# A graph layer pair on one core: load order at the start, gathers one group earlier, rows moved from the edge loop to the node stage, destinations of the attention stage by six bits, and sums on GpSimd in the last stage

## The chip, the cores and the metric

The kernel runs on one core of a Trainium2 chip, in one launch. Its time is device microseconds; the median of three runs stands for a kernel. One further execution was profiled, and all durations below come from that one. Engines are named as in the profile: PE (TensorE), PEld (its weight loads), DVE (VectorE), ACT (ScalarE), POOL (GpSimd), SP (the queue that issues most DMAs).

## What is computed

6250 nodes of 128 features, 100,000 edges sorted by destination. First a message layer, then an attention layer, each with a residual and a layer norm:

```python
edge_features = concat([x[src], x[dst], gaussians(edge_weight)])
h = silu(edge_features @ Wm1 + bm1)
h = silu(h @ Wm2 + bm2)
out = segment_sum(h @ Wm3 + bm3, dst)
u = silu(concat([x, out]) @ Wu1 + bu1) @ Wu2 + bu2
x = layernorm(x + silu(u @ Wi1 + bi1) @ Wi2 + bi2)
xt = logmap0(x)
att = sigmoid(concat([xt[src], xt[dst], edge_attr_128]) @ att_w.T + att_b)
support = xt + segment_sum(xt[src] * att, src) + mean_by_src(edge_attr_128) + mean_by_dst(edge_attr_128)
x = layernorm(x + proj(expmap0(support)))
```

## The kernel before

`window_path` is the whole kernel; a second path exists for inputs that don't fit its windows and isn't run. The order of the instructions on each engine is written out by hand: every engine works through its own list, and waits on semaphores of the others. Edges go in 98 groups of 1024 (`NG`), a group in four windows of 256 and eight blocks of 128 edges.

**Start.** SP loads x in nine pieces (L889), ACT's queue the source and destination indices (L894), POOL's queue 17 weights and biases (L699, `later`, issued in one go). 13 rounds of four node blocks each are turned (L1014) and multiplied (L1033) once for `p_src`, once more for `p_dst`, the projections of all nodes; between them DVE works through `pieces`, a list that makes gather indices, window bases and low bits out of the raw indices.

**Edge loop** (L1270 on), two halves per group. `gather` (L1087) fetches the group's rows of `p_src` by eight indirect DMAs on POOL, two groups ahead of their use; 16 are issued before the loop. `layer1`, `layer2` and `sum_up` are the products (L1204, L1207, L1221, L1236). Rows of edge attributes have to be added by source node as well, and for this the kernel sorts them: `scatter` (L818) writes a block's 128 attribute rows by an indirect DMA into tables in HBM that have room for every block of 128 nodes (buckets). Of a group's eight blocks two are scattered in the edge loop (`early`, blocks 0 to 2), except that every fifth group leaves one of them for later (`left`, 20 groups); before its first scatter POOL waits for a copy of the low bits by ACT (`attr_row`, L1324).

**Node stage.** 13 rounds of four node blocks run the update network. `move_middle` scatters the third of blocks 0 to 2 of each group and then what `left` kept back, three rows a call: three SP loads, one to three ACT copies (L1359), three scatters. Each round calls it three times; what is left over comes after the rounds. After them a serial chain on DVE (L1476 to L1516) makes the logarithmic map's scale and `a_t`, the two dot products of every node with the attention weights. The destination's dot products are laid out for look-up as `w3`: for each of 392 windows, which begins at any node, a column of 128 values. Products with 0/1 matrices `up` fetch them out of `a_t` (L1526), a choice by `second` (is the low part of the base above the partition?) joins the two node blocks that a window reaches into (L1528 to L1531), and a loop splits it in three bf16 parts (L1533, L1535).

**Attention.** 98 iterations. In each, for group `it`: `logits` multiplies what was looked up with `hi` (`pick`, L1686), reduces it (L1687), adds the edge's own part (L1688), and ACT makes the sigmoids (L1689, L1692). `move` issues five scatters on POOL (L818) of blocks 3 to 7, whose rows now carry the sigmoid. `one_hots(it + 1)` makes `ohT` (L1663), a bf16 0/1 matrix of 128 partitions x 2048 columns: for each of 1024 edges the low seven bits of its source, then of its destination, compared with the partition number; and `hi` (L1665), which picks the node block. `look_up(it + 1)` has TensorE multiply them: for each of the eight blocks three products with the three parts of the source's table (L1677) and one with `w3` (L1679). The low bits arrive by one DMA of 512 KB that repeats a row of HBM over 128 partitions (`load_lo`, L1386). Beside that, sums of finished buckets are made from the tables (loads L1589, one-hots L1602, products L1618, `add` L1629), by a plan that spreads them over the iterations.

**Last stage.** Nine loads of the last buckets (`load(k)`, L1589, into four places, two used twice at first), for each `so_far` (L1794), one-hots (L1602), products (L1804), means (L1823), `xp` on POOL (L1830), its reduction (L1834); then, for blocks 0 to 23 and 24 to 48, `finish`: small products of 24 or 25 columns, and per block `scaled` on ACT (L1883), `added` on DVE (L1887) and a store for every six blocks.

Of the kernel before, what the change touches and what calls it, by code (L numbers as in the profile page):

```python
# [531 lines left out]
W = 64  # L532
# [17 lines left out]
def left(g):  # L550

    return (1, 2, 0)[g % 3] if g % 5 == 0 else None
# [50 lines left out]
def window_path(ctx, tc, bad, x, src, dst, edge_attr, edge_weight, Wm1, bm1, Wm2, bm2, Wm3, bm3,  # L603
# [49 lines left out]

    const = ctx.enter_context(tc.tile_pool(name="const", bufs=1))
# [36 lines left out]

    noff = const.tile([P, 1], F32, name="noff")
    nc.vector.tensor_scalar(noff, part, -float(KR), -STEP, op0=OP.add, op1=OP.mult)

# [3 lines left out]
    def later(t, w):  # L698
        waiting.append(lambda: nc.gpsimd.dma_start(t, w))  # L699
# [48 lines left out]

    wm3 = weight(Wm3, "wm3")
# [10 lines left out]
    later(bi2x, bi2[None, :].to_broadcast([P, F]))  # L760
    bi2p = const.tile([P, 4, F], BF16, name="bi2p")
# [11 lines left out]
    keep = ctx.enter_context(tc.tile_pool(name="keep", bufs=1))  # L773

# [9 lines left out]
    acc = keep.tile([P, 3, ROWS], F32, name="acc")  # L784
# [51 lines left out]
    egat = of_edges.enter_context(tc.tile_pool(name="egat", bufs=4, reuse_waits="tile"))  # L836
# [37 lines left out]
    with tc.tile_pool(name="init", bufs=1) as init, \  # L874
            tc.tile_pool(name="initw", bufs=3) as initw, \
            tc.tile_pool(name="initp", bufs=2, space=PSUM) as initp:

        xs = acc[:, 0, :NB * F].rearrange("p (r f) -> p r f", f=F)
        xT = acc[:, 2, :NB * P].rearrange("f (r p) -> f r p", p=P)
        XL = N - (P - 1) * NB  # L880
        xv = x[:(P - 1) * NB].rearrange("(p r) f -> p r f", r=NB)
        nc.vector.memset(xs[96:, XL:], 0.0)
# [4 lines left out]
        nc.vector.memset(raw[R0:, 1, TAIL:], -1)  # L887
        for lo, hi in ((0, 8), (8, 24), (24, NB)):
            nc.sync.dma_start(xs[:112, lo:hi], xv[:112, lo:hi])  # L889
            nc.sync.dma_start(xs[112:P - 1, lo:hi], xv[112:, lo:hi])  # L890
            nc.sync.dma_start(xs[P - 1:, lo:min(hi, XL)],
                              x[(P - 1) * NB + lo:(P - 1) * NB + min(hi, XL)][None])
        for s, v in enumerate((src, dst)):
            nc.scalar.dma_start(raw[:R0, s], v[:R0 * GE].rearrange("(g e) -> g e", e=GE))  # L894
            nc.scalar.dma_start(raw[R0:NG - 1, s], v[None, R0 * GE:(NG - 1) * GE])
            nc.scalar.dma_start(raw[NG - 1:, s, :TAIL], v[None, (NG - 1) * GE:])
        for f in waiting:
            f()
        for t in (p_src, p_dst):
            nc.sync.dma_start(t[NB * P:], zrow[:, :F])  # L900
        nc.sync.dma_start(first_t[(NB - 1) * LO:NB * LO].rearrange("(p r) f -> p r f", p=P),
                          zrow[:, None, :RW].to_broadcast([P, LO // P, RW]))
        nc.vector.memset(acc[:, 1], 0.0)
# [82 lines left out]
        def lower(s):  # L986
# [5 lines left out]
        pieces = [  # L992
# [6 lines left out]
            bases, spread, relative, lambda: turn(1), lambda: upper(0), lambda: upper(1), rest, begins,  # L999
            lambda: bias_rows(init, bm2x, bm2p),  # L1000
            lambda: nc.vector.tensor_copy(beside[:, 1:], attw),
            copy_lws,
            lambda: nc.vector.tensor_single_scalar(raw, raw, P - 1, OP.bitwise_and)]
# [17 lines left out]
        for s in range(2):  # L1021
            if s:
                load(0)
                load_attr(0)
                load(1)
            for r, (b0, nb) in enumerate(rounds):
                if s == 0:
                    turn_x(r + 1)
                if r % 2 == 0:
# [15 lines left out]
                if s or r >= 3:  # L1045
                    for _ in range(1):
                        if pieces:
                            pieces.pop(0)()
        for p_ in pieces:
            p_()  # L1050
        for s in range(2):
            lower(s)
# [5 lines left out]
    with tc.tile_pool(name="ework", bufs=2, reuse_waits="tile") as ework, \  # L1058
# [5 lines left out]

        counts = ework.tile([P, 2, NB], F32, name="counts", bufs=1)
# [14 lines left out]
        def gather(g, bs):  # L1080
            if g >= NG:
                return
            if g not in gas:
                gas[g] = egat.tile([P, 8, F], F32, name="ga")
# [193 lines left out]
        extra = {12: turn, 14: multiply, 16: lambda: bias_rows(ework, bi2x, bi2p)}  # L1278
# [3 lines left out]
        for g in range(2):  # L1282
# [6 lines left out]
        for g in range(NG + 2):  # L1289
            for half in range(2):  # L1290
# [10 lines left out]
                gather(g + 2, range(4 * half, 4 * half + 4))  # L1301
# [72 lines left out]

    w3 = stat.tile([P, 4 * NG, 3], BF16, name="w3")
# [7 lines left out]
    def load_lo(g):  # L1383
        if g < NG:
            los[g] = aload.tile([P, 2, 8, P], BF16, name="los")
            nc.sync.dma_start(los[g].rearrange("p s b e -> p (s b e)"),  # L1386
                              row_lo[g].rearrange("s e -> (s e)").partition_broadcast(P))

    with tc.tile_pool(name="nwork", bufs=2, reuse_waits="tile") as nwork, \
# [15 lines left out]
        up = nwork.tile([P, 2, NW], F32, name="up", bufs=1)  # L1405
        nc.vector.tensor_single_scalar(bits, base_w, P - 1, OP.bitwise_and)
        nc.vector.tensor_copy(bits_f, bits)
        nc.vector.tensor_scalar(second, bits_f, part, None, op0=OP.is_gt)
        nc.vector.tensor_single_scalar(bits, base_w, 7, OP.arith_shift_right)
        nc.vector.tensor_copy(bits_f, bits)  # L1410
        for q in range(2):
            nc.vector.tensor_scalar(up[:, q], bits_f, float(q), part, op0=OP.add, op1=OP.is_equal)
# [107 lines left out]
        a_up = stat.tile([NB, P], F32, name="a_up")  # L1520
        nc.vector.tensor_copy(a_up, pt[:NB, 0])
# [3 lines left out]
        for q, t in enumerate(two):  # L1525
            nc.tensor.matmul(t, lhsT=a_up, rhs=up[:NB, q], start=True, stop=True)  # L1526
# [5 lines left out]
        for q in range(3):  # L1532
            nc.vector.tensor_copy(w3[:, :, q], w_a)  # L1533
            if q < 2:
                nc.vector.tensor_sub(w_a, w_a, w3[:, :, q])  # L1535

# [35 lines left out]
    with tc.tile_pool(name="bwork", bufs=2, reuse_waits="tile") as bwork:  # L1572
# [58 lines left out]
        with tc.tile_pool(name="awork", bufs=2, reuse_waits="tile") as awork, \  # L1631
# [26 lines left out]
            def one_hots(g):  # L1658
# [3 lines left out]
                ohT = awork.tile([P, 2, 8, P], BF16, name="ohT")  # L1662
                nc.vector.tensor_scalar(ohT, los.pop(g), part, None, op0=OP.is_equal)  # L1663
# [320 lines left out]
```

## Time and profile before

| | us |
|---|---|
| median of three runs | 2843.29 (2835.01 to 2847.82) |
| profiled execution | 2827.59, its span 2825.8 |
| start, to the first layer-1 product | 0 to 68 |
| edge loop | 68 to 1683 |
| node stage | 1683 to 1886 |
| attention | 1886 to 2741 |
| last stage | 2741 to 2825.8 |

The mean granted TensorE clock of that execution was 0.754. A row of the profile names line, engine, operation, output and inputs by the program's names, and, in square brackets, how long the engine stood before it and what let it go; "issue" stands for a wait for nothing that the profile shows. The costliest groups, as count, busy time and mean duration:

```profile
L1087 POOL DMA_INDIRECT ga<-p_src,src_i x782 | 758.5, 970 | 261.6 <-issue 230.4
L818 POOL DMA_INDIRECT late<-attr,to_i x298 | 290.2, 974 | 253.0 <-ACT att L1692 143.5
L818 POOL DMA_INDIRECT early<-attr_row,to_i x176 | 175.5, 997 | 458.3 <-ACT attr_row L1324 269.6
L1677 PE MATMUL pg<-a,ohT 128*128 128x49 bf16 x2346 | 137.3, 199 | 200.2 <-DVE ohT L1663 102.6
```

A row reads: line, engine, operation, output and inputs, count; then busy time in us and mean duration in ns; then the idle time before, and what ended most of it.

### The profile page before, as it was taken

The page shows a single profiled execution, that of the slowest core. Times are in us where ns is not written, and L with a number is a line of the kernel's source. Part 1 is how long each engine was busy: PE and PEld are TensorE (multiplying, and loading weights), DVE is VectorE, ACT ScalarE, POOL GpSimd, SP SyncE. Part 2 cuts the span into 40 slices and gives each one's busy share as a digit, 9 for nine tenths or more (in the row PEclk, how much of TensorE's full clock was granted, in tenths as well). Part 3 has the DMA queues.
Part 4 walks back from the last instruction along what each step waited for, and adds up shares of the span by engine and source line. Part 5 has one row for each costly group of instructions (what it writes and reads, how often), then busy time and mean ns, then how long its engine had stood idle before and what let it go on. Part 6 is the DMA issues. An engine that isn't in the chain of part 4 may idle for free. (4 is left out here: it accounts for less than half of the span.)

```text
span 2825.8 us, 41692 instructions
## 1 busy us (share of the span) xinstructions
PE 1935.6 (68%) x13353; PEld 1678.1 (59%) x13353; DVE 1656.1 (59%) x4438; ACT 915.8 (32%) x1576; POOL 1550.3 (55%) x1608
## 2 busy tenths in 40 slices
PE   6567677776777675767777786746666776766674
PEld 5456566665666565656666673425555766666663
DVE  6466665666666555655666663444444555555668
ACT  3445444444444444444344431111111110000005
POOL 4556555555555555555655546545555555555542
PEclk8788878878777777878787786756666777676877
DMA  7445454454444444444433433446666666766743
GB/s 215 111 123 147 127 129 125 124 132 127 123 128 119 121 122 119 121 112 123 106 98 103 110 85 108 122 126 196 190 198 201 207 214 204 226 191 218 230 149 104
DMA packets 349749, 412.11 MB, mean 146 GB/s; under 512 B 53701, under 2 KB 265931, under 8 KB 349265
## 3 DMA queue, kind: packets, MB, share of 16 engines
q1 hardware_dynamic: 298168, 303.00, 37.9%
q0 software_dynamic: 50624, 105.02, 12.3%
q8 instruction: 108, 1.77, 0.3%
q10 hardware_dynamic: 728, 1.33, 0.2%
q14 instruction: 121, 0.99, 0.1%
HBM read 319.13 MB, written 90.00 MB: 145 GB/s over the span
## 5 line engine op out<-in xcount | busy, mean ns | idle before, releaser
L1087 POOL DMA_INDIRECT ga<-p_src,src_i x782 | 758.5, 970 | 261.6 <-issue 230.4
L1252 DVE TENSOR_TENSOR acc<-acc,ps 128x192 f32 x391 | 138.3, 354 | 511.2 <-remote 253.5
L818 POOL DMA_INDIRECT late<-attr,to_i x298 | 290.2, 974 | 253.0 <-ACT att L1692 143.5
L818 POOL DMA_INDIRECT early<-attr_row,to_i x176 | 175.5, 997 | 458.3 <-ACT attr_row L1324 269.6
L1618 PE MATMUL pb<-acc,oh 128*128 128x130 f32 x1764 | 348.5, 370 | 34.8 <-issue 33.9
L1236 PE MATMUL ps<-hot,h 128*128 128x64 f32 x1564 | 320.9, 285 | 73.7 <-issue 71.9
L1618 PEld LDWEIGHTS pb<-acc,oh 128*128 128x128 f32 x1764 | 322.4, 278 | 46.3 <-issue 45.7
L1210 ACT ACTIVATE h<-pa,bm1c 128x512 f32<-128x512 f32 x196 | 134.7, 687 | 648.1 <-remote 212.0
L1221 PEld LDWEIGHTS pb<-wm,h 128*128 128x128 f32 x1564 | 258.7, 232 | 102.7 <-issue 77.4
L1236 PEld LDWEIGHTS ps<-hot,h 128*128 128x128 f32 x1564 | 266.6, 211 | 75.4 <-issue 73.9
L1207 PE MATMUL pa<-feat,lw 128*128 128x256 f32 x782 | 278.4, 486 | 40.5 <-issue 38.6
L1221 PE MATMUL pb<-wm,h 128*128 128x128 f32 x1564 | 259.3, 313 | 50.7 <-issue 49.6
L1677 PE MATMUL pg<-a,ohT 128*128 128x49 bf16 x2346 | 137.3, 199 | 200.2 <-DVE ohT L1663 102.6
L1677 PEld LDWEIGHTS <-ohT 128*128 128x128 bf16 x2346 | 113.4, 105 | 232.5 <-DVE ohT L1663 115.1
L1238 PE MATMUL ps<-hot,attr 128*128 128x64 f32 x976 | 204.3, 286 | 54.6 <-issue 53.8
L1686 DVE TENSOR_TENSOR pick<-pg,hi 128x416 f32<-128x416 f32 x98 | 57.8, 590 | 309.3 <-remote 161.8
L1207 PEld LDWEIGHTS pa<-feat,lw 128*128 128x128 f32 x782 | 177.5, 250 | 82.0 <-issue 60.1
L1204 PE MATMUL pa<-ident,ga 128*128 128x128 f32 x782 | 162.8, 327 | 88.1 <-issue 52.1
L1238 PEld LDWEIGHTS ps<-hot,attr 128*128 128x128 f32 x976 | 161.6, 204 | 54.3 <-issue 53.9
L1223 ACT ACTIVATE h<-pb 128x512 f32<-128x512 f32 x196 | 116.4, 594 | 229.7 <-remote 111.7
L1204 PEld LDWEIGHTS pa<-ident,ga 128*128 128x128 f32 x782 | 113.2, 169 | 103.3 <-issue 75.2
L1689 ACT ACTIVATE attr<-lg,attb 128x5 f32<-128x5 f32 (+1 forms) x60 | 18.3, 305 | 412.9 <-DVE lg L1688 411.3
(343 smaller groups left out, 3995.5 us busy)
## 6 DMA issues: line engine op xcount, KB each, us to landing
los<-row_lo SPq DMA_DIRECT2D x98, 512.0 KB
near<-in_edge_weight_dram SPq DMA_DIRECT2D x97, 256.0 KB
attr<-in_edge_attr_dram SPq DMA_DIRECT2D x97, 256.0 KB
acc<-late SPq DMA_DIRECT2D x38, 528.0 KB
late<-zrow SPq DMA_DIRECT2D x22, 792.0 KB
acc<-early SPq DMA_DIRECT2D x49, 330.0 KB
attr<-in_edge_attr_dram SPq DMA_DIRECT2D x247, 64.0 KB
attr<-in_edge_attr_dram SPq DMA_DIRECT2D x118, 128.0 KB
```

Source lines behind the costliest of these rows:

```text
L818: nc.gpsimd.indirect_dma_start(out=t, out_offset=bass.IndirectOffsetOnAxis(ap=to_i[:, b, g:g + 1], axis=0), in_=rows_, in_offset=None)
L1087: nc.gpsimd.indirect_dma_start(out=gas[g][:, b], out_offset=None, in_=p_src[:, :], in_offset=bass.IndirectOffsetOnAxis(ap=src_i[:, b, g:g ...
L1204: nc.tensor.matmul(pa[:, j], lhsT=gas[g][:, 2 * k0 + j], rhs=ident, is_transpose=True, start=j == 0, stop=False)
L1207: nc.tensor.matmul(pa[:, 2 * k:2 * k + 2], lhsT=lws[(4 * g + k0 + k) % NL], rhs=feats[g][:, k0 + k], start=False, stop=k == kk - 1)
L1210: nc.scalar.activation(hid1[i][:, :2 * kk], pa[:, :2 * kk], AF.Silu, bias=bm1c)
L1221: nc.tensor.matmul(pb[:, j], lhsT=h1[:, j], rhs=wm2, start=False, stop=j == nb - 1)
L1223: nc.scalar.activation(hid2[i][:, :nb], pb[:, :nb], AF.Silu)
L1236: nc.tensor.matmul(ps[:, k, 0], lhsT=h2[:, 2 * k + c], rhs=hot[:, b], start=k == 0 and c == 0, stop=False)
L1238: nc.tensor.matmul(ps[:, k, 1], lhsT=head[:, b, :F] if b < 3 else rest[:, b - 3], rhs=hot[:, b], start=False, stop=False)
L1252: nc.vector.tensor_add(acc[:, :, bass.ds(at, W)], acc[:, :, bass.ds(at, W)], ps[:, k])
L1618: nc.tensor.matmul(pb[:, h], lhsT=oh[:, a + h, j], rhs=bt[:, a + h, j, :S], start=j == 0 and h == 0, stop=j == c - 1 and h == n - 1)
L1677: nc.tensor.matmul(pg[:, b, :NB], lhsT=ohT[:, 0, b], rhs=a3[q], start=q == 0, stop=q == 2)
```

## The change

Five parts in one step.

1. **Start and loads.** x and the indices all go on SP, the first two thirds of x, then the source indices, the rest of x, the destination indices. POOL's weight loads begin once the last column of x has landed (`gate`); eleven that only the node stage needs go to SP in the edge loop (`at_ease`), and the products of weights that use them move to half-groups 52 to 56. `pieces` falls into two lists, one per pass over the nodes; the first two groups' loads move behind most of the second pass.
2. **Gathers** run three groups ahead, with six buffers for four; 24 come before the loop.
3. **`left`** keeps one block back in 33 groups (g mod 9 in 0, 4, 8) for 20: 163 scatters in the edge loop for 176, 131 in the node stage for 118.
4. **Attention by six bits.** The destination's low bits become six, so 64 partitions serve one edge and the two halves of the partitions serve two: `los` and `ohT` have 12 blocks for 16. Three DMAs bring 256 and twice 64 KB; `ohT` is made in two parts with `hi` between them; `w3` has columns in which the other half is zero, and `up` and `a_up` double.
5. **Last stage.** Four loads stand up front; `added` of blocks 0 to 17 goes to POOL, six blocks in two instructions; the last 25 blocks begin with block 48, and DVE scales every third of them.

The diff, cut to its core (of the order of the loads and of moved lines only what is spoken of):

```diff
-    return (1, 2, 0)[g % 3] if g % 5 == 0 else None
+    return (1, 2, 0)[g % 3] if g % 9 in (0, 4, 8) else None
...
+        def indices(i):
+            v = (src, dst)[i]
+            nc.sync.dma_start(raw[:R0, i], v[:R0 * GE].rearrange("(g e) -> g e", e=GE))
+            nc.sync.dma_start(raw[R0:NG - 1, i], v[None, R0 * GE:(NG - 1) * GE])
+            nc.sync.dma_start(raw[NG - 1:, i, :TAIL], v[None, (NG - 1) * GE:])
         for lo, hi in ((0, 8), (8, 24), (24, NB)):
             nc.sync.dma_start(xs[:112, lo:hi], xv[:112, lo:hi])
             nc.sync.dma_start(xs[112:P - 1, lo:hi], xv[112:, lo:hi])
             nc.sync.dma_start(xs[P - 1:, lo:min(hi, XL)],
                               x[(P - 1) * NB + lo:(P - 1) * NB + min(hi, XL)][None])
-        for s, v in enumerate((src, dst)):
-            nc.scalar.dma_start(raw[:R0, s], v[:R0 * GE].rearrange("(g e) -> g e", e=GE))
-            nc.scalar.dma_start(raw[R0:NG - 1, s], v[None, R0 * GE:(NG - 1) * GE])
-            nc.scalar.dma_start(raw[NG - 1:, s, :TAIL], v[None, (NG - 1) * GE:])
...
+        gate = init.tile([1, 1], F32, name="gate")
+        nc.gpsimd.tensor_copy(gate, xs[:1, NB - 1, :1])
         for f in waiting:
-            f()
-        for t in (p_src, p_dst):
-            nc.sync.dma_start(t[NB * P:], zrow[:, :F])
-        nc.sync.dma_start(first_t[(NB - 1) * LO:NB * LO].rearrange("(p r) f -> p r f", p=P),
-                          zrow[:, None, :RW].to_broadcast([P, LO // P, RW]))
-        nc.vector.memset(acc[:, 1], 0.0)
+            f(nc.gpsimd)
...
+        ga_tiles += [ework.tile([P, 8, F], F32, name=f"ga{i}", bufs=1) for i in (4, 5)]
...
-        extra = {12: turn, 14: multiply, 16: lambda: bias_rows(ework, bi2x, bi2p)}
+        extra = {52: turn, 54: multiply, 56: lambda: bias_rows(ework, bi2x, bi2p)}
 
         load_rows(0)
         load_rows(1)
-        for g in range(2):
+        for g in range(3):
             gather(g, range(8))
...
+                if at_ease and i % 4 == 2 and i > 4:
+                    at_ease.pop(0)(nc.sync)
+                    assert i < 50
+                gather(g + 3, range(4 * half, 4 * half + 4))
...
-            los[g] = aload.tile([P, 2, 8, P], BF16, name="los")
-            nc.sync.dma_start(los[g].rearrange("p s b e -> p (s b e)"),
-                              row_lo[g].rearrange("s e -> (s e)").partition_broadcast(P))
+
+            los[g] = aload.tile([P, 12, P], BF16, name="los")
+            nc.sync.dma_start(los[g][:, :8].rearrange("p b e -> p (b e)"), row_lo[g, 0].partition_broadcast(P))
+            for h in range(2):
+                nc.sync.dma_start(los[g][h * W:(h + 1) * W, 8:].rearrange("p b e -> p (b e)"),
+                                  row_lo[g, 1, h * GE // 2:(h + 1) * GE // 2].partition_broadcast(W))
...
-        up = nwork.tile([P, 2, NW], F32, name="up", bufs=1)
-        nc.vector.tensor_single_scalar(bits, base_w, P - 1, OP.bitwise_and)
+        up = nwork.tile([P, 2, 2, NW], F32, name="up", bufs=1)
+        nc.vector.tensor_single_scalar(bits, base_w, W - 1, OP.bitwise_and)
         nc.vector.tensor_copy(bits_f, bits)
-        nc.vector.tensor_scalar(second, bits_f, part, None, op0=OP.is_gt)
-        nc.vector.tensor_single_scalar(bits, base_w, 7, OP.arith_shift_right)
+        nc.vector.tensor_scalar(second, bits_f, part64, None, op0=OP.is_gt)
+        nc.vector.tensor_single_scalar(bits, base_w, 6, OP.arith_shift_right)
         nc.vector.tensor_copy(bits_f, bits)
         for q in range(2):
-            nc.vector.tensor_scalar(up[:, q], bits_f, float(q), part, op0=OP.add, op1=OP.is_equal)
+            for i in range(2):
+                nc.vector.tensor_scalar(up[:, q, i], bits_f, float(q), twice[:, i:i + 1],
+                                        op0=OP.add, op1=OP.is_equal)
...
-        a_up = stat.tile([NB, P], F32, name="a_up")
-        nc.vector.tensor_copy(a_up, pt[:NB, 0])
+
+        a_up = stat.tile([NB, 2, 2, W], F32, name="a_up")
+        nc.vector.tensor_copy(a_up, pt[:NB, 0].rearrange("h (i l) -> h i l", l=W)[:, :, None].to_broadcast(
+            [NB, 2, 2, W]))
         a3 = split3(node, a_t[:, 0], [P, NB], "a3")
         two = [npp.tile([P, 4, P], F32, name=n).rearrange("p a b -> p (a b)")[:, :NW]
                for n in ("pm", "pw")]
         for q, t in enumerate(two):
-            nc.tensor.matmul(t, lhsT=a_up, rhs=up[:NB, q], start=True, stop=True)
+            for i in range(2):
+                nc.tensor.matmul(t, lhsT=a_up[:, i].rearrange("h s l -> h (s l)"), rhs=up[:NB, q, i],
+                                 start=i == 0, stop=i == 1)
...
+        for h in range(2):
+            nc.vector.memset(w3[h * W:(h + 1) * W, (1 - h) * 2 * NG:(2 - h) * 2 * NG], 0.0)
...
-                ohT = awork.tile([P, 2, 8, P], BF16, name="ohT")
-                nc.vector.tensor_scalar(ohT, los.pop(g), part, None, op0=OP.is_equal)
+                ohT = awork.tile([P, 12, P], BF16, name="ohT")
+                lo = los.pop(g)
+                nc.vector.tensor_scalar(ohT[:, :8], lo[:, :8], part, None, op0=OP.is_equal)
                 hi = hi_t[g % 3]
                 nc.vector.tensor_tensor(
                     hi[:, :n, :NB], cols_p[:, None, :NB].to_broadcast([P, n, NB]),
                     hif[:, 0, :n, g, None].to_broadcast([P, n, NB]), op=OP.is_equal)
+                nc.vector.tensor_scalar(ohT[:, 8:], lo[:, 8:], part64, None, op0=OP.is_equal)
                 hot[g] = ohT, hi
...
-                        nc.tensor.matmul(pg[:, b, :NB], lhsT=ohT[:, 0, b], rhs=a3[q],
+                        nc.tensor.matmul(pg[:, b, :NB], lhsT=ohT[:, b], rhs=a3[q],
                                          start=q == 0, stop=q == 2)
-                    nc.tensor.matmul(pg[:, b, NB:], lhsT=ohT[:, 1, b], rhs=w3[:, b // 2 * NG + g],
+                    nc.tensor.matmul(pg[:, b, NB:], lhsT=ohT[:, 8 + b % 4], rhs=w3[:, b // 2 * NG + g],
                                      start=True, stop=True)
...
+                def added_by_pool(c0, c1):
+                    t = sup[:, c0:c1]
+                    nc.gpsimd.tensor_tensor(t, t, fac[:, c0 - b0:c1 - b0, None].to_broadcast([P, c1 - c0, F]),
+                                            op=OP.mult)
+                    nc.gpsimd.tensor_tensor(x1[:, c0:c1], x1[:, c0:c1], t, op=OP.add)
+                    store(c0, c1)
...
-                if k > HC + 3:
-                    add_some(CB)
+                    if n_scaled < H:
+                        pool_some(CB)
...
+            blocks = [NB - 1] + list(range(H, NB - 1))
+            own = [i % 3 == 2 for i in range(len(blocks))]
+            for b, own_ in zip(blocks, own):
+                if not own_:
+                    scaled(b)
+            since = H
+            for i, (b, own_) in enumerate(zip(blocks, own)):
+                if own_:
+                    scaled(b, True)
                 added(b)
```

## The prediction, made before the changed kernel ran

> **What bounds the kernel now.** I read the time by stage first (busy time of each engine in five stretches), then the costliest groups, then the timeline of single iterations.
>
> ```profile
> core 0: us, PE busy (x) PEld busy (x) DVE busy (x) ACT busy (x) POOL busy (x), PEclk, DMA share, GB/s
> 0.00:68.00 68.00, 42.49 (x276) 39.41 (x276) 46.27 (x116) 27.00 (x41) 31.08 (x52) 0.88 0.74 220
> 68.00:1683.00 1615.00, 1144.13 (x6945) 1000.51 (x6945) 996.80 (x2900) 725.72 (x888) 914.76 (x941) 0.79 0.44 119
> 1683.00:1886.00 203.00, 130.64 (x418) 71.94 (x418) 80.54 (x263) 33.84 (x97) 114.78 (x118) 0.68 0.39 113
> 1886.00:2741.00 855.00, 577.39 (x5442) 531.41 (x5442) 465.85 (x902) 87.21 (x392) 474.52 (x488) 0.69 0.65 202
> 2741.00:2825.80 84.80, 41.00 (x275) 34.86 (x274) 66.64 (x260) 42.06 (x158) 15.17 (x10) 0.76 0.39 118
> ```
>
> No engine is full in the two long stages (edges 1615 us, attention 855 us): both are paced by hand-overs. One attention iteration shows how:
>
> ```profile
> 2267.23 0.17 DVE L1688 TENSOR_TENSOR lg<-lg,ew 128x8 f32<-128x8 f32 x1
> 2267.32 0.75 DVE L1663 TENSOR_SCALAR ohT<-los,part 128x2048 bf16<-128x2048 bf16 x1
> ...
> 2267.98 0.56 DVE L1665 TENSOR_TENSOR hi<-beside,hif 128x392 bf16<-128x392 f32 x1
> ...
> 2268.10 0.96 POOL L818 DMA_INDIRECT late<-attr_last,to_i  x1 [3.40 <-ACT att L1692]
> ...
> 2268.12 0.31 PE L1677 MATMUL pg<-a,ohT 128*128 128x49 bf16 x3 [3.11 <-DVE ohT L1663]
> ...
> 2273.18 0.97 POOL L818 DMA_INDIRECT late<-attr_last,to_i  x1 [0.30 <-issue]
> 2275.32 0.59 DVE L1686 TENSOR_TENSOR pick<-pg,hi 128x416 f32<-128x416 f32 x1 [4.30 <-PE pb L1618]
> ```
>
> The look-up (24 products L1677, 8 products L1679) is over by 2269.5, yet `pick`, which needs only that, starts at 2275.32: after GpSimd's run of five scatters (2268.10 to 2274.15). In this trace other engines' signals hang while GpSimd issues indirect DMAs back to back: in the edge loop TensorE's share of time stalled on "issue" is 0.01 in the first 2 us of such a run, 0.3 at 8 to 10 us, 0.8 beyond 16. So an iteration is the run (6.06 us), some 1.2 us of release, and 2.1 us of pick, reduce, lg and ScalarE up to the next scatter: 9.4 us. The iterations do take 6.4, 7.8, 9.4 or 10.3 us, mean 8.7. Where the look-up ends 0.97 to 1.41 us into the run (51 iterations), `pick` is let go inside the run in about 36 of them; where it ends later than 2.2 us, hardly ever. That is the hinge of this change.
>
> **Start.** Node loads ahead of indices and weights: the last of x lands 11.4 us in, while 0.8 MB of indices and 17 weights share the queues. The first gather waits for p_src (last store issued 40.43, gather 43.59), 13 projection rounds that DVE and TensorE pace; only the head of that moves. POOL's weights now wait for x, but POOL stood 22.69 us before that gather, which covers them. I take -2. Bounds: -6 (half the time to the last x), and +8 if nine loads in a row on SP and the later destination indices hold up DVE's pieces.
>
> **Edge loop.** (a) Gathers three groups ahead: TensorE reads a gather 15 to 51 us after it lands and waits 4.6 us for gathers in all, so nothing is to be had. It costs at the start: 8 more gathers by 0.96 + 0.30 us = 10 us ahead of the first scatter. That one is at 75.87; the second waited 13.23 us idle until 95.18, which covers the scatters, but the run under which TensorE and ScalarE stall grows by 10 us: +5 (0 to +10). (b) 33 instead of 20 groups leave one scatter for later: 176 to 163. At 0.997 + 0.30 us that is 16.9 us of GpSimd, but GpSimd idles a third of this stage. The kernel before already leaves one in every fifth group: such a group and the one before it take 12.1 + 19.8 = 31.9 us, two others 2 x 16.2 = 32.4. A scatter that goes lets two runs of four gathers grow together. So 0.5 us each: -6.5; the ends are -17 and +8 (two such groups now stand side by side). (c) Eleven weight loads on SP and the later weight products fall where neither SP nor TensorE is last: 0. Together -1.5.
>
> **Node stage.** The 13 scatters come back behind the loop, with four more moves (131 scatters against 118). GpSimd is idle there from 1865.4 to 1890.05, so 13 x 1.27 = 16.5 us fit; but they run beside the serial DVE chain of 1868 to 1886, which has four hand-overs to ScalarE or TensorE, and the copies for them now stand in ScalarE's order beside its square root. I take +5 (0, if no signal hangs, to +13). On that same chain lies the six-bit table: pairs of fp32 products L1526 become fours,
>
> ```profile
> 1877.93 1.67 PE L1526 MATMUL pm<-up,a_up 49*128 49x392 f32 x2 [0.38 <-DVE a_up L1521]
> 1879.40 1.51 PE L1526 MATMUL pw<-up,a_up 49*128 49x392 f32 x2
> ```
>
> that is +1.5 +1.5, and two memsets of w3 by about 0.25: +3.5. Nothing hides this. Stage: +8.5.
>
> **Attention.** The packed destinations: `ohT` of 2048 columns becomes 1024, then `hi`, then 512. From 0.75 us for 2048 with about 0.1 fixed I take 0.43 and 0.27: DVE's sum stays what it was, and DVE isn't full. The look-up starts 0.3 us earlier but its fourth product waits for the second part, which ends near +0.4 us of the run instead of `ohT` at -0.04; 31 products follow it instead of 32. So its end moves by +0.15 to +0.3 us. From the 51 iterations: those ending at 0.97 to 1.08 had a mean period of 7.39 us (17), those at 1.26 to 1.41 7.67 (32), 0.28 us for 0.35 us. With 0.23 us, 0.18 x 51 = +9. The bounds: every iteration at 9.4 gives 98 x 9.4 - 855 = +66; -15 if the smaller load (384 KB for 512 KB, at a DMA share of 0.65) or the earlier start lets the long ones go. SP gets two more issues by about 0.5 us in an iteration where its five issues take some 3.3 of 8.7 us: covered.
>
> A rule speaks against the second part. The Trainium skill, "SBUF — State Buffer", section "Who interferes with whom", says that a DVE tensor_scalar in a two-port mode takes the port pair that GpSimd writes its descriptors through, and that the loser stands still for the whole instruction. The trace has it, but not always:
>
> ```profile
> 2069.01 1.32 POOL L818 DMA_INDIRECT late<-attr,to_i  x1 [0.30 <-issue]
> ...
> 2069.47 0.75 DVE L1663 TENSOR_SCALAR ohT<-los,part 128x2048 bf16<-128x2048 bf16 x1
> ```
>
> Here a scatter took 1.32 instead of 0.97. In the edge loop DVE's L1114 (0.47 us) starting 0.05 to 0.36 us into a gather left it at 0.955; starting at -0.16 or at +0.45 it made it 1.15 or 1.05. The second part would lie at about +0.05 to +0.35 of the first scatter, a free place. By the rule: 0.3 x 98 = +29 us; by the rows 0. I take 0 and keep 29 for the range.
>
> **Last stage.** Four loads up front take most of a wait (L1602 at 2753.02 stood 3.53 us for a load): -3. `added` of 18 blocks goes to GpSimd; 12 stood in DVE's loop and took 3.23 + 1.88 = 5.1 us:
>
> ```profile
> 2792.83 2.19 DVE L1887 SCALAR_TENSOR_TENSOR x<-acc,fac,x 128x128 f32<-128x128 f32 x2
> ...
> 2793.06 1.81 POOL L1830 TENSOR_TENSOR xp<-acc,x 128x768 f32<-128x768 f32 x1 [1.43 <-DVE acc L1823]
> ```
>
> The same section says that a DVE instruction with two SBUF inputs also loses to a GpSimd one that reads SBUF: the second `added` here did, two took 2.19 instead of 0.54. But `oh` (L1602, two SBUF inputs too) kept its 1.75 beside `xp`, seven times. GpSimd gets six more instructions of 1.82 us. By the rule up to 10.9 us of DVE stand; by L1602 none, but the small products from 2800.36 on are like `added`, and two GpSimd instructions can lie there: 3.6. And `reduce` waits for `xp` behind them in GpSimd's order, about 2. (SP's stores now wait for GpSimd; the last bucket load is issued two steps before the first of them, so only stores queue behind.) So -5.1 + 5.6 = +0.5. The end: 25 scalings on ScalarE take 9.73 us; shared with DVE (25 x 0.27 + 8 x 0.2 = 8.3) -1.4; the last store is a third as large, -0.6. Stage: -4.5 (-9 to +4).
>
> **Sum.** -2 -1.5 +8.5 +9 -4.5 = +9.5. The profiled execution took 2827.59 us (span 2825.8 and 1.8 around it), so 2837 of its own; it lay 0.55% below the median of 2843.29. On the median: 2853.
>
> **Rivals.** *Attention loses its short iterations (slower).* The second part's signal to TensorE falls 0.4 us inside the run, where the first left before it. If the look-up's end thereby crosses the point (somewhere between +1.41 and +2.25 us) up to which `pick` is let go inside the run, all go to 9.4 us: +66, with the other parts 2910; half of them, +35, 2879. For it: 36 of 51 hang on less than 0.9 us, and DVE's signals were late by half a microsecond in such runs. Against: my shift is 0.3 at most.
> *The scatters pay in full (faster).* If the edge loop gains 16.9 for 13 scatters, the longer first run costs nothing, the start gives -4, the last stage -7, and only the table's 3.5 us stays: -24, 2819. For it: scatters are what GpSimd waits in front of (269.6 us on ScalarE's row copies). Against: the 31.9 to 32.4 above.
> *Nothing moves beyond the measurement.* That is the sum above: small terms of both signs.
>
> **Chances.** What a measurement of this kernel can tell from no change is about 0.5%, 14 us. Forecast (about +10, within 2830 to 2857): 0.31. Attention loses short iterations, in part or all (2858 to 2910): 0.37. Edge and ends pay (2790 to 2829): 0.32. The range leaves out the last tenth on each side: 2802 to 2898.
>
> **What would show it.** Look at the periods of `pick`: as many of 6.4 and 7.8 as before, or 9.4 throughout. TensorE's first L1679 product should wait on the second `ohT`. First scatters of a run at 0.97 us show the free place, 1.3 the rule. In the edge loop the period by group shows whether a group with its scatter left makes the next one longer; TensorE's "issue" rows show the same. From a_t to the first `ohT` should take 9 + 3.5 us. In the last stage the DVE wait at the first `oh` should go, and DVE rows near 1.9 us beside GpSimd's sums show the port. I'm wrong at the root if attention shortens though the look-up ends later: then the signal isn't what lets `pick` go.

## The result, and the profile after

| | before | changed | ratio |
|---|---|---|---|
| median of 20 runs, us | 2839.85 (2815.28 to 2850.58) | 2872.44 (2834.02 to 2906.11) | 1.0092 (1.0063 to 1.0122) |
| profiled execution, us | 2827.59 | 2865.24 | |

The changed kernel is slower by 0.9%. The ratio is of fast executions alone, those within 1.5% of the fastest of the same kernel, while the medians are of all 20 and stand 1.15% apart. The experiments were made in five sets, each with the kernel before measured in it. In four sets that kernel took 2158 to 2159 us instead of 2840, in one 2827. So the runs below fall in two conditions, and a ratio is always taken inside one set.

The first view is busy time by engine in the stages of the changed kernel (the columns are those of the table shown for the kernel before):

```profile
66.60:1691.00 1624.40, 1133.79 (x6946) 993.46 (x6944) 996.68 (x2901) 729.97 (x894) 894.07 (x924) 0.80 0.44 118
1691.00:1913.00 222.00, 153.98 (x429) 82.94 (x427) 82.95 (x268) 34.90 (x109) 126.34 (x130) 0.61 0.37 111
1913.00:2776.00 863.00, 594.45 (x5430) 546.59 (x5431) 459.92 (x992) 85.69 (x389) 471.24 (x485) 0.68 0.62 185
2776.00:2863.40 87.40, 42.68 (x286) 35.83 (x284) 67.32 (x258) 39.50 (x153) 27.72 (x19) 0.77 0.38 117
```

I read the stage bounds from single events: the first layer-1 product, the last product of `sum_up`, the first DVE reciprocal of `rstd`, the first `ohT`, the last `pick`.

| stage, us | before | changed | difference | predicted |
|---|---|---|---|---|
| to the first layer-1 product | 66.8 | 66.6 | -0.2 | -2 |
| edge loop | 1615.8 | 1624.7 | +8.9 | -1.5 |
| node rounds | 188.4 | 201.3 | +12.9 | 0 |
| serial chain to the first `ohT` | 14.7 | 20.2 | +5.5 | +8.5 |
| attention | 848.6 | 862.9 | +14.3 | +9 |
| last stage | 91.5 | 87.8 | -3.7 | -4.5 |
| span | 2825.8 | 2863.4 | +37.6 | +9.5 |

**Start.** The first gather came at 35.74 instead of 43.59. Yet the first layer-1 product didn't move. Timeline of TensorE and its loads, changed kernel:

```profile
47.74 1.16 PE L1065 MATMUL pj<-wm1n,acc 128*128 128x128 f32 x8 [1.63 <-ACT pj_sb L1071]
51.19 2.08 PE L1065 MATMUL pj<-wm1n,acc 128*128 128x128 f32 x8 [2.29 <-issue]
65.24 0.79 PE L1065 MATMUL pj<-wm1n,acc 128*128 128x128 f32 x2 [11.97 <-issue]
...
88.01 1.36 PEld L1235 LDWEIGHTS pa<-feat,lw 128*128 128x128 f32 x4 [20.79 <-issue]
```

The last projections stand 2.3 and 12.0 us, and a weight load of the first layer 20.8 us, for nothing that the profile names. GpSimd issues gathers back to back meanwhile. In the kernel before the longest such stall of a weight load in these groups is 10.3 us, at 80.04. What the earlier loads gave, these stalls took.

**The chain.** Timeline of TensorE and DVE after the node rounds:

```profile
1900.97 2.98 PE L1566 MATMUL pm<-up,a_up 49*128 49x392 f32 x4 [1.78 <-DVE a_t L763]
1903.75 2.82 PE L1566 MATMUL pw<-up,a_up 49*128 49x392 f32 x4
...
1911.35 0.55 DVE L1579 MEMSET w<- 64x588 bf16 x1 [0.18 <-DVE w L1574]
1912.06 0.55 DVE L1579 MEMSET w<- 64x588 bf16 x1 [0.16 <-issue]
```

The products are 1.3 us longer each than before (2.98 for 1.67, 2.82 for 1.51), the wait ahead of them is 1.4 us longer, beside a run of 14 scatters (1885.9 to 1903.4), and the two memsets take 1.4 us: together 5.4 of the 5.5 us.

**Attention.** One iteration, timeline of DVE, GpSimd and TensorE:

```profile
2263.22 0.48 DVE L1708 TENSOR_SCALAR ohT<-los,part 128x1024 bf16<-128x1024 bf16 x1
...
2264.00 0.97 POOL L837 DMA_INDIRECT late<-attr_more,to_i  x1 [3.58 <-ACT att L1738]
2264.09 0.34 DVE L1713 TENSOR_SCALAR ohT<-los,part 128x512 bf16<-128x512 bf16 x1
...
2264.49 0.19 PE L1725 MATMUL pg<-w,ohT 128*128 128x3 bf16 x1 [0.49 <-DVE ohT L1713]
...
2269.32 0.97 POOL L837 DMA_INDIRECT late<-attr_more,to_i  x1 [0.30 <-issue]
2271.26 0.59 DVE L1732 TENSOR_TENSOR pick<-pg,hi 128x416 f32<-128x416 f32 x1 [4.35 <-PE pb L1662]
```

As before, `pick` starts 7.26 us after the run began (2264.00), though the look-up was done by 2265.8. New is the fourth product's wait for the second part of `ohT`. Over 96 iterations of each trace, by when the look-up's last product ended, counted from the first scatter of the run (two of before and three of the changed kernel, which ended before 0.9, are left out):

| look-up's end, us | before: count, mean period | changed: count, mean period |
|---|---|---|
| 0.9 to 1.15 | 17, 7.39 | none |
| 1.15 to 1.5 | 32, 7.67 | 19, 7.98 |
| 1.5 to 2.2 | none | 39, 8.10 |
| 2.2 to 4 | 19, 9.26 | 13, 9.68 |
| over 4 | 26, 10.15 | 22, 10.32 |

The modes moved from 0.97 and 1.41 to 1.37 and 1.75. Periods of 6 to 7 us fell from 21 to 16.

**Last stage.** Timeline of GpSimd and DVE at the second `finish`:

```profile
2837.03 1.47 POOL L1939 TENSOR_TENSOR acc<-acc,fac 128x768 f32<-128x768 f32 x1
2837.30 1.23 DVE L1889 TENSOR_TENSOR f<-f,s_log 128x25 f32<-128x25 f32 x1
...
2838.57 1.85 POOL L1941 TENSOR_TENSOR x<-x,acc 128x768 f32<-128x768 f32 x1
2838.79 1.67 DVE L1892 TENSOR_TENSOR h<-h,tx 128x25 f32<-128x25 f32 x1
```

Products of 25 columns, 0.17 to 0.19 us before, take 1.23 and 1.67: each ends when GpSimd's instruction does. That is 2.5 of the 3.6 us put down for the port.

### The profile page after: what moved, and what is told of

Same layout as the page of the kernel before. It is cut to its first block, busy times and chain, and to the rows that moved or that the text cites. A ratio compares the mean times of both kernels' runs of the same rounds, so it can differ in the third digit from the quotient of the medians.

```text
span 2863.4 us, 42768 instructions
## 1 busy us (share of the span) xinstructions
PE 1963.9 (69%) x13357; PEld 1694.4 (59%) x13357; DVE 1652.6 (58%) x4535; ACT 912.9 (32%) x1581; POOL 1549.6 (54%) x1604
## 4 chain that ended last, share of the span: by engine, by line
PE 35%; DVE 26%; issue 16%; another core or an unknown queue 15%; ACT 3%; DMA 3%; DVEq 1%; SPq 1%; POOL 0%; ACTq 0%; POOLq 0%
PE pb L1662 7%; PE pa L1235 5%; PE pb L1249 4%; PE ps L1266 3%; PE pg L1723 3%; PE ps L1264 3%; PE pa L1232 2%; DVE acc L1280 2%; PE pS L1757 2%; DVE oh L1646 2%; DVE prod L1217 2%; DVE pick L1732 1%; DVE lg L1733 1%; DVE prods L1165 1%
## 5 line engine op out<-in xcount | busy, mean ns | idle before, releaser
L837 POOL DMA_INDIRECT early<-attr_row,to_i x164 | 163.9, 1000 | 485.8 <-ACT attr_row L1355 231.4
L1662 PE MATMUL pb<-acc,oh 128*128 128x130 f32 x1764 | 361.9, 380 | 42.8 <-issue 41.4
L1662 PEld LDWEIGHTS pb<-acc,oh 128*128 128x128 f32 x1764 | 336.3, 288 | 51.9 <-issue 51.1
L1249 PE MATMUL pb<-wm,h 128*128 128x128 f32 x1564 | 250.9, 310 | 18.1 <-issue 17.3
```

Of the source, the lines that this page charges most:

```text
L837: nc.gpsimd.indirect_dma_start(out=t, out_offset=bass.IndirectOffsetOnAxis(ap=to_i[:, b, g:g + 1], axis=0), in_=rows_, in_offset=None)
L1249: nc.tensor.matmul(pb[:, j], lhsT=h1[:, j], rhs=wm2, start=False, stop=j == nb - 1)
L1662: nc.tensor.matmul(pb[:, h], lhsT=oh[:, a + h, j], rhs=bt[:, a + h, j, :S], start=j == 0 and h == 0, stop=j == c - 1 and h == n - 1)
```

## The experiments

Theory A is the one of the prediction: other engines' signals hang while GpSimd issues a run, and what ends later in a run is let go later. The rivals stand in each expectation.

**Six bits alone** (parts of the diff: `los`, `ohT`, `up`, `a_up`, `w3`, on the kernel before).

> The six-bit destinations alone, on the kernel before. Theory A (the look-up ends 0.35 to 0.4 us later in GpSimd's run of scatters, because its fourth product waits for the second part of ohT, and fewer picks are let go inside the run): the look-up ends 1.37 and 1.75 us into the run instead of 0.97 and 1.41, attention (first ohT to last pick) 848.6 -> about 863 us, the chain from rstd to the first ohT 14.7 -> about 19 us, the rest as before; the time 2840 -> about 2859. Rival B (the six bits are innocent in attention; its 14 us there were the luck of one profile or follow from the other parts): attention stays within 5 us of 848.6, the time rises by 4 us at most.

Measured: 2147.58 against 2159.18 us, ratio 0.9955 (0.9941 to 0.9969): faster. Attention took 614.2 us and the chain 19.1. Neither theory had this, and both had reckoned from a kernel of 2840 us.

**`ohT` in two halves alone**, seven bits:

```diff
-                nc.vector.tensor_scalar(ohT, los.pop(g), part, None, op0=OP.is_equal)
+                lo = los.pop(g)
+                nc.vector.tensor_scalar(ohT[:, 0], lo[:, 0], part, None, op0=OP.is_equal)
                 hi = hi_t[g % 3]
...
+                nc.vector.tensor_scalar(ohT[:, 1], lo[:, 1], part, None, op0=OP.is_equal)
```

> The kernel before with ohT made in two halves (sources, then destinations, 1024 columns each) and hi between them; seven bits, one load, the same table. Theory A: the look-up ends as late as with six bits or 0.1 us later still, attention 848.6 -> 863 to 867 us, everything else as before, so +14 to +18 us. Rival C (it is the three loads a group, or the smaller table's products, that cost): attention stays at 848 within 5 us.

Measured: 0.9968 (0.9957 to 0.9979), attention 620.8 us. No theory had foreseen a gain.

**33 groups leaving a scatter, alone** (the one line of `left`).

> 33 instead of 20 groups leave a scatter, on the kernel before. Theory A (a scatter that goes joins two runs of gathers, so the edge loop gains next to nothing, and the node stage pays for all of them): edge loop within 8 us of 1615.6, node stage 203.3 -> 213 to 219 us, of which some 2 on the serial chain after the rounds and the rest in the rounds; the time +8 to +16. Rival D (the edge loop gains the 13 scatters' GpSimd time): edge loop -13 to -17 us, the time -5 or better.

Measured: 0.9939 (0.9927 to 0.9952), edge loop 1184.9 us (1202.2 in the next run, which leaves it alone), rounds 151.0, chain 15.5. Rival D holds here: 13 scatters by 1.27 us are 16.5.

**The last stage's part alone.**

> The last stage's part alone: four loads up front, GpSimd's sums, scalings shared with DVE. Theory A: from the last pick to the end 91.5 -> 87 to 88 us, the rest unchanged, the time -4 (inside the measurement). Rival E (the gain there came from other data in the tables' places or chance): 91 to 92 us.

Measured: 0.9997 (0.9989 to 1.0005), last pick to end 100.2 us. No change: kernels without this part have 98.7 to 101.0 us in this condition, and DVE stands 11.0 us there for the first late bucket load with the part and (in the run with two halves) without it.

The kernel before took 2159 us beside all four. So I looked at what differs in those traces. In the one of the last stage's part, where all earlier stages are as before, TensorE's share of time stalled on "issue" is 0.00 through the first 30 us of GpSimd's run, and in the edge loop nine of ten signals of DVE, ScalarE and TensorE are seen within 0.01 us of the end of their instruction. In the first profile of before that point lies at 3.5, 10.3 and 6.2 us, as far as the trace has the signals (a lost record looks like a late one), though half of DVE's and ScalarE's signals are seen within 0.1 us there too. GpSimd never rests in the later trace: there are 953 indirect DMAs up to the last gather with 1.5 us of extra gaps in all, where the first profile of before has 385 us in 92 gaps. A period of an attention iteration is 6.4 us, GpSimd's five scatters. I call this condition *signals in time*, the other *signals late*.

The granted TensorE clock goes with the condition: 0.73 to 0.76 in every execution with late signals whose clock is on record, 0.84 to 0.87 in those of the other kind but one. A slow TensorE is thus a rival. The one exception speaks against it, an execution of the kernel with `left` alone: at a clock of 0.631 it took 2240 us, so a lower clock alone doesn't make 2830.

**The changed kernel again, and look-up two iterations ahead** (`one_hots(it + 2)` and `look_up(it + 2)` for `it + 1`, a fourth `hi` buffer).

> The changed kernel once more, unaltered. In the last four runs the kernel before took 2159 us instead of 2840, TensorE stood nowhere on 'issue', and edge loop and attention ran at GpSimd's own pace (12.3 us a group, 6.4 us an iteration). Theory F: the change's sign hangs on whether signals are late during GpSimd's runs. Where they aren't, the parts add up: edge -17 (13 scatters less), attention -14, chain +4 to +5, node rounds +2 to +8, last stage 0, start 0: 2159 -> 2131 to 2141, ratio about 0.989. Where they are late (the kernel before near 2840), the ratio is 1.009 again. Rival G: the result was a matter of the kernel and not of such a state; the ratio is 1.009 here too.

> The kernel before with one-hots and look-up of attention made two iterations ahead of their use instead of one (a fourth hi buffer). It takes the wait of pick for a look-up of the same run away. Where signals are late: if the look-up's signal is what holds pick, the iterations fall from 8.7 us towards GpSimd's own 6.4, attention 848 -> 640 to 720 us and the time 2840 -> 2640 to 2720; if pick is held by something else (the bucket products, the run itself), attention stays above 820. Where signals aren't late, attention is at GpSimd's pace already (628 us for 98 x 6.4) and gains 0 to 10 us.

Measured, signals in time (before 2159.03): the changed kernel 2127.73 us, ratio 0.985 (0.9832 to 0.9868), faster by 1.5%; Theory F stands, Rival G is out. Look-up ahead: 1.0002 (0.9992 to 1.0011), attention 626.7 us, which says nothing on late signals. The stages of the changed kernel in that profile, edge loop and attention:

```profile
54.30:1241.00 1186.70, 983.47 (x6948) 873.94 (x6946) 1002.23 (x2902) 723.38 (x891) 899.60 (x934) 0.91 0.61 162
...
1413.00:2028.00 615.00, 470.33 (x5416) 441.68 (x5416) 467.70 (x993) 85.70 (x389) 465.30 (x476) 0.79 0.88 262
```

The work of GpSimd (900 and 465 us) and of DVE (1002 and 468) is what it was, in 1187 and 615 us instead of 1624 and 863. TensorE is busy for less (983 for 1134 us, 470 for 594) at a higher clock (0.91 for 0.80, 0.79 for 0.68). And GpSimd's groups of scatters:

```profile
L837 POOL DMA_INDIRECT late<-attr,to_i x298 | 291.3, 978 | 99.4 <-issue 64.3
...
L837 POOL DMA_INDIRECT early<-attr_row,to_i x164 | 164.1, 1001 | 50.0 <-issue 36.9
```

The idle time before them is 0.33 and 0.30 us each, close to the 0.30 us that lie between any two DMAs of a run; the page of the kernel before had 253.0 and 458.3 us there.

What then shortens attention by six bits, if no look-up is waited for? The scatters themselves. Timeline of DVE and GpSimd, kernel with the last stage's part alone (so the whole `ohT`):

```profile
1704.79 0.75 DVE L1663 TENSOR_SCALAR ohT<-los,part 128x2048 bf16<-128x2048 bf16 x1 [1.31 <-DMA los<-row_lo]
...
1705.17 1.22 POOL L818 DMA_INDIRECT late<-attr,to_i  x1 [0.30 <-issue]
```

and the changed kernel:

```profile
1706.20 0.97 POOL L837 DMA_INDIRECT late<-attr,to_i  x1 [0.30 <-DMA late<-attr_more,to_i]
1706.52 0.34 DVE L1713 TENSOR_SCALAR ohT<-los,part 128x512 bf16<-128x512 bf16 x1
```

A scatter of 0.97 us takes 1.22 when the long comparison lies over its start: the rule on the port that I had weighed and set to zero. With the shorter parts fewer scatters are held up, and for less time each. The sum over the 488 scatters of each trace follows attention:

| kernel | scatters over 1.0 us | their excess, us | attention, us |
|---|---|---|---|
| whole `ohT` (last stage's part alone) | 83 | 18.3 | 627.9 |
| two halves, seven bits | 79 | 9.8 | 620.8 |
| six bits, both parts ahead of `hi` | 57 | 6.9 | 617.8 |
| six bits alone | 40 | 4.3 | 614.2 |
| changed kernel | 40 | 4.1 | 615.0 |

From the first row to the last the excess falls by 14.2 and attention by 12.9 us.

**Both parts ahead of `hi`; the start alone; gathers alone.**

```diff
                 nc.vector.tensor_scalar(ohT[:, :8], lo[:, :8], part, None, op0=OP.is_equal)
+                nc.vector.tensor_scalar(ohT[:, 8:], lo[:, 8:], part64, None, op0=OP.is_equal)
                 hi = hi_t[g % 3]
...
-                nc.vector.tensor_scalar(ohT[:, 8:], lo[:, 8:], part64, None, op0=OP.is_equal)
```

> The changed kernel with both parts of ohT made ahead of hi. Theory H (where GpSimd's stream of indirect DMAs never pauses, attention is 488 scatters by 1.27 us plus what DVE's two-port comparisons hold up: 83 long scatters and 18 us with the whole ohT, 40 and 4 us with the split one): the order moves where the two comparisons fall in a scatter; the long scatters change in number, attention follows their sum within 3 us, and stays between 609 and 630 us. If signals are late in this call (the kernel before near 2840): by Theory A the look-up ends some 0.4 us earlier again, and attention loses 10 to 15 us of its 863. Rival: the place of hi doesn't matter, 615 +-2 (or 863 +-5).

> The start's part alone (x and indices on SP, weights after x, eleven weights in the edge loop), gathers two ahead. Where signals are in time: the first gather 42.5 -> 36 us, the first layer-1 product 66.5 -> 54 to 60, the edge loop unchanged at 1202, so the end of the last gather and the time come 6 to 7 us earlier, 2159 -> 2152. Rival: the first product comes early only with 24 gathers ahead; then 66. Where signals are late: first gather at 36, first product still near 66, no gain.

> Gathers three groups ahead alone. Where signals are in time GpSimd's stream is the bound and the same 953 DMAs lie in it, in another order: the same time within 3 us, unless TensorE's waits for gathers (100 us in the first four runs of these) now go and the edge loop's tail shortens: up to -5. Where signals are late: +0 to +10 from the longer first run.

Measured, signals in time (before 2158.67): parts first 0.9859 (0.984 to 0.9879), attention 617.8 us. Against the changed kernel the excess grows by 2.8 us and attention by 2.8, within the 3 us that Theory H gave. The start alone 0.9932 (0.9915 to 0.995), first product at 54.0 us; with 13.5 us of the whole time it gave twice what I had expected from the first gather's 6 to 7. The last gather ended 10.8 us earlier than in the run with the last stage's part alone, so about 4 us come from inside the loop; from where, I haven't traced. Gathers alone 0.9981 (0.9973 to 0.9989), within the expected -5 to +3.

**Two tensors compared in the edge loop**, on the changed kernel.

```diff
-            nc.vector.tensor_scalar(feat[:KR, k0:k1], nd[:, k0:k1], part[:KR], None, op0=OP.is_equal)
+            nc.vector.tensor_tensor(feat[:KR, k0:k1], nd[:, k0:k1],
+                                    part[:KR, :, None, None].to_broadcast([KR, k1 - k0, 2, P]), op=OP.is_equal)
```

> The changed kernel, with the destination one-hots of the edge loop (0.47 us comparisons with a scalar) written as a comparison of two tensors. Theory H (GpSimd's stream is the bound, and DVE's scalar comparisons hold up its descriptor writes): of 940 DMAs before the last gather some 50 were longer than 1.02 us, 8.9 us in all; they fall below 10, and the edge loop 1187 -> 1177 to 1180 us, the time 2128 -> 2118 to 2121, ratio near 0.981. Rival: the long ones come from something else (the queue's own restarts): as many stay, and the time doesn't move. Where signals are late the stream pauses anyway, and the time stays at that of the changed kernel.

Measured: this set met late signals. Before took 2827.3 us on a chip of the same number that had given 2159.03 two sets earlier; this kernel took 2873.33, ratio 1.0139 (1.0086 to 1.0192), an interval that overlaps the changed kernel's. So the loss of the changed kernel came back with the condition, and its stages with it: edge loop 1620.8, rounds 198.8, chain 20.3, attention 857.0, last stage 88.6. The expectation on the port failed: 83 DMAs over 1.02 us instead of 59, 25.0 us instead of 11.2.

```profile
325.19 0.68 DVE L1142 TENSOR_TENSOR feat<-near,part 64x512 f32<-64x512 bf16 x1
...
325.52 1.17 POOL L1115 DMA_INDIRECT ga<-p_src,src_i  x1 [0.30 <-PE pb L1250]
```

A comparison of two tensors holds a gather up too, and longer, as it lasts 0.68 instead of 0.47 us.

**Six bits and `left`, once more**, for the late condition.

> The six-bit destinations alone again, for the state in which signals are late (the last run met it: the kernel before took 2827 us there, on a chip that had taken 2159 shortly before). In that state Theory A: attention 848.6 -> 858 to 865 us, the look-up's end at 1.37 and 1.75 us of the run, chain 14.7 -> 19 to 20 us, the time +14 to +20 (ratio 1.005 to 1.007). Rival: attention within 5 us of 848, ratio below 1.003; then the loss of the whole change lies in the edge loop and the node rounds. In the other state: ratio 0.9955 as before.

> 33 groups leaving a scatter, alone, again for the state with late signals. Theory A there: edge loop 1608 to 1620 us (1615.8 before), node rounds 188 -> 194 to 202 us, chain within 2 us, the time +5 to +14 (ratio 1.002 to 1.005). Rival D: the edge loop gains 13 to 17 us and the time falls. In the other state: ratio 0.994 as before.

Measured: signals were in time again (before 2158.01). Ratios 0.9951 (0.9937 to 0.9964) and 0.9958 (0.9944 to 0.9973), stages as in the first two of the kind (attention 614.7; edge loop 1185.3). They repeat the earlier runs and leave the parts' shares under late signals untried.

## Why the prediction was right or wrong

The time lay in the range, at 2872 instead of 2853. It lay outside the forecast's own band (2830 to 2857, chance 0.31), in the band of the case that had the highest chance (0.37), that attention loses short iterations. That the number fell there is in part luck: of the 28 us by which the profiled difference passed the forecast (37.6 for 9.5), attention gave 5, the edge loop 10 and the node rounds 13.

**What the runs show of the cause.** The change's sign follows the condition, not the kernel: 1.0092 with late signals, 0.985 with signals in time. With signals in time GpSimd's unbroken stream of DMAs is the bound in the edge loop and in attention, and a part gives what it takes out of that stream or by how much it lets it begin earlier: the start 0.7%, `left` 0.4 to 0.6%, six bits 0.5%, gathers 0.2%, the last stage nothing. These add up to 1.8 to 2.0% where the whole change gave 1.5%, so they overlap. With late signals GpSimd stands in gaps, 385 us in the edge loop before and 417 after. That work taken from it then buys nothing, and that what the change adds on the way (later signals, longer runs, a longer chain) is paid, is my reading of the stages; the parts were not tried alone there.

**Attention** (+9 predicted, +14.3). The first steps of the mechanism are in the trace: second part at +0.09 us of the run, look-up's end later, fewer short periods. The mis-sized term is the shift: 0.23 us assumed, 0.34 to 0.40 measured, since the parts took 0.48 and 0.34 us and not 0.43 and 0.27 (0.75, 0.48 and 0.34 us leave 0.2 that doesn't shrink with the size, for the 0.1 assumed). By the slope used, 0.28 us per 0.35, a shift of 0.4 on 58 iterations is +19. But the slope isn't confirmed: inside the changed kernel's own trace the two early groups stand at 7.98 and 8.10, in the variant's at 8.26 and 7.95, and in the changed kernel the late ones grew as well. No run isolates this under late signals: one profile of the changed kernel (862.9) and one of its variant (857.0) stand against one of before.

**The port** (0 by the rows, 29 by the rule). Under late signals right: 93 of 96 second parts lay in a scatter that kept 0.96 to 0.97 us. What I missed is that the rule has a price for the whole `ohT` too, 18 us of attention with signals in time. Under late signals the scatters over 1.0 us of the kernel before lose 1.2 us in all.

**Node stage** (+8.5, measured +18.4). The step that failed is the +5 for the 13 scatters beside the serial chain. The longer wait that stands beside them on the chain is 1.4; the table's products and memsets cost 4.0 for 3.5 (with signals in time six bits alone have a chain of 19.1 us for 14.8). The other 12.9 us lie in the rounds, where I had put none. With signals in time `left` alone has rounds of 151.0 and 151.3 us, where kernels without it have 143 to 149, so 2 to 8 us of it are the moves; the rest is seen in two profiles under late signals (201.3, 198.8) and not explained.

**Edge loop** (-1.5, measured +8.9 and, in the variant, +5.0). "0.5 us each" for 13 scatters failed. By position in nine, groups 8 and 1 of the changed kernel take 21.9 and 11.1 us, the others 15.0 to 17.6; the mean over the loop is 16.4 us in both kernels. The pattern that I had priced is there, and it yields nothing. The +5 for the longer first run was right in kind: TensorE stood 20.8 us at 88.01, the summing products of the second group begin 9.7 us later than before, and those of the last group still 8.7. In the variant they begin 15.9 us later and one group on 0.9 us earlier, so single profiles don't fix the size.

**Start** (-2, measured -0.2). The head moved by 7.9 us, more than I gave it; the run of gathers took it back. With signals in time it is worth 13.5 us.

**Last stage** (-4.5, measured -3.7; with signals in time 0). Under late signals the sum was near, but not by its terms. The port's stall was there (2.5 for 3.6). DVE's waits for bucket loads ahead of its one-hots, put down as -3, still came to 3.1 us (1.69, 0.78 and 0.60) for 3.5, and the reduction stood 5.1 us behind GpSimd's sums for the 2 assumed. What made up for it I haven't worked out.

**What stays open.** What makes signals late, and whether the lower clock is a part of the cause or follows from it. It is no property of the kernel, and not of a chip of one number; no run here could set it. Nor is it tried whether making the look-up two iterations ahead helps where it should, under late signals.

## What to carry to other kernels

Ask what an engine's freed time buys: 13 scatters less shortened the edge loop by 17 us where GpSimd's stream never paused, and the loop was no shorter where the stream stood in gaps behind late signals. A profile of one execution may show a condition of the moment and not of the kernel; a second profile of the kernel before, at another time, could have turned this forecast's sign. A cost that a wait hides (here the comparison over a scatter, 18 us) comes to light only in the condition without the wait.

## What the runs showed of the hardware

The same program took 2159 and 2827 us on a chip of the same number in two sets of measurements. In the long condition TensorE's share of time stalled on "issue" rises with the age of GpSimd's run of indirect DMAs (edge loop, changed kernel: 0.01 in the first 2 us, 0.36 at 8 to 10, 0.53 at 16 to 18; in the kernel before beyond 16 us it is 0.55, and not the 0.8 of the prediction), and the packets of the DMA queues take the same time in both (median 0.033 us on GpSimd's queue, kernel before and kernel with the last stage's part alone).

A DVE comparison holds up an indirect DMA by when it lies, not by being there: one of 0.75 us starting 0 to 0.2 us ahead of a scatter made it 1.41 us in the median, one starting 0 to 0.2 us after its start left it at 0.98 (kernel with the last stage's part alone). In steps of 0.1 us, with 5 to 16 cases each, the medians of that trace are 1.43 for a comparison starting 0.1 to 0.2 us ahead, 0.97 for one less than 0.1 us ahead, 1.30 for one starting 0.4 to 0.5 us after the scatter's start, and 0.97 in the next step. The Trainium skill, "SBUF — State Buffer", section "Who interferes with whom", has the loser stand for the whole instruction, and two-input DVE instructions contend only with GpSimd instructions that read SBUF. If an indirect DMA, which takes its indices from SBUF, counts as one that reads, both comparisons below should hold it up, and if it doesn't, neither. The measurement decides: the two-input comparison of the edge loop made gathers 1.36 us in the median when it started up to 0.2 us ahead of them, while the two-input `oh` of attention (1.08 us) left scatters at 0.97 in the median wherever it lay. Why the two differ isn't shown.
